# Six fields of the second tile loaded in parts of 39, 40 and 49 rows, and later loads in two pieces of 8 KB

## The chip, the cores and the metric

One core of a Trainium2 chip runs the kernel. The metric is the device time of one execution in microseconds, lower being better. The time before is 1293.61 us (median of 3 runs, 1291.99 to 1294.53). Other chips give the same kernel medians up to 1297.1 us, so every comparison below is with runs of the kernel before on the same chip in the same rounds. Where a kernel has a single run, its time is used only as a hint.

## The reference

```python
def _L0_rec_ref(x, W):                       # x: 4096 x 32 x 64, W: 64 x 64, float32
    vid = jnp.einsum('bfd,de->bfe', x, W)
    idx_i, idx_j = jnp.triu_indices(32, k=1)  # 496 pairs i < j
    return x[:, idx_i, :] * vid[:, idx_j, :]  # 4096 x 496 x 64, 520 MB
```

One small matrix product, then 496 products of fields for each sample. The input is 33.6 MB, the output 520 MB.

## The kernel before

The batch is cut into 16 tiles of 256 samples: 128 partitions, 32 fields, 128 columns. TensorE makes `vid` in PSUM, VectorE multiplies into output tiles of 124 pairs, and SyncE's queue stores each of these. A full store is one transfer of 128 rows of 63,488 B.

```python
    xpool = ctx.enter_context(tc.tile_pool(name="x", bufs=2))
    opool = ctx.enter_context(tc.tile_pool(name="out", bufs=3))
    ...
    def load(t, pieces, queue):
        xt = xpool.tile([P, F, C], F32, tag="x", name=f"x_{t}")
        n = F // pieces
        for lo in range(0, F, n):
            queue.dma_start(out=xt[:, lo : lo + n, :], in_=x[t][:, lo : lo + n, :])
        return xt

    loaded = [load(0, 4, nc.sync), load(1, 2, nc.sync)]
    ...
    for t in range(NT):
        if 0 < t < NT - 1:
            loaded.append(load(t + 1, 4, nc.scalar))
        xt = loaded[t]
        ...  # matmuls of the tile into PSUM
        for at, m, w, i, di, j, dj in products(by_field() if t < 2 else by_block()):
            ...
            nc.vector.tensor_tensor(o, left, right, ALU.mult)
            at += n
            if t * NP + at == until or at in (base + SLOT, NP):
                nc.sync.dma_start(
                    out=out[t][:, sent:at, :],
                    in_=ot[:, sent - base : at - base, :],
                )
```

The first two tiles are loaded on SyncE's queue. From tile 2 on ScalarE's queue loads the next tile as soon as an x buffer is free, in four pieces of 8 fields, 4 KB per partition.

## Time and profile before

| | before |
|---|---|
| median time, us | 1293.61 |
| profiled span, us | 1293.4 |
| bytes moved, MB | 553.8 |
| VectorE busy | 84% |
| DMA engines busy | nine tenths or more in 39 of 40 slices |

The table of DMA issues below (transfer, issuing queue, count, KB of one, median us from issue to landing) shows that a store waits behind another one, as it lands in 43 us but takes 20, and that a load piece needs about as long in the median:

```profile
out_dram<-o SPq DMA_DIRECT2D x56, 7936.0 KB, 43.1
x<-in_r_x_dram ACTq DMA_DIRECT2D x56, 512.0 KB, 45.5
```

The **excess** of a store packet is its duration above the 2342 ns that undisturbed packets of 63,488 B take. The **lag** of a DMA engine is how long after the first of the 16 engines it finishes the same store, read from the 16 completion writes. The **spread** is the lag of the last engine at the last store. Packet durations and completion writes are in the DMA records of each trace.

### The profile page before, as it was taken

How to read it: one execution, taken by the hardware profiler on the slowest of the kernel's cores; microseconds unless marked ns; L12 is line 12 of the kernel's file. 1: busy time of each engine (PE TensorE's matmuls, PEld its weight loads, DVE VectorE, ACT ScalarE, POOL GpSimd, SP SyncE). 2: the span in 40 equal slices, each digit the busy share in tenths (PEclk: the TensorE clock that was granted, in tenths of full speed). 3: DMA queues.
4: the chain of work that ended last, by engine and by line, in shares of the span. 5: the costliest groups of instructions: out<-in, count | busy, mean ns of one | idle time of the engine just before them, and what ended most of it. 6: DMA issues, size and time to landing. Idle time of an engine off the chain costs nothing.

```text
span 1293.4 us, 1789 instructions
## 1 busy us (share of the span) xinstructions
PE 227.8 (18%) x512; PEld 48.5 (4%) x512; DVE 1083.6 (84%) x320; POOL 0.2 (0%) x4
## 2 busy tenths in 40 slices
PE   4112122112122121221212212122121221212000
PEld 1000000000000000000000000000000000000000
DVE  7999999888898887888879788798887988979870
POOL 0000000000000000000000000000000000000000
PEclk7555555555555565555555556555565555555555
DMA  9999999999999999999999999999999999999996
GB/s 393 429 423 438 429 432 435 430 431 434 433 434 431 432 433 435 433 435 436 433 431 436 431 433 431 435 434 431 431 431 434 431 433 427 427 431 438 438 430 302
DMA packets 20889, 553.80 MB, mean 428 GB/s; under 512 B 2448, under 2 KB 2448, under 8 KB 10256
## 3 DMA queue, kind: packets, MB, share of 16 engines
q1 hardware_dynamic: 12816, 524.33, 93.9%
q10 hardware_dynamic: 8064, 29.36, 5.6%
q8 instruction: 4, 0.07, 0.0%
q14 instruction: 5, 0.04, 0.0%
HBM read 33.59 MB, written 520.09 MB: 428 GB/s over the span
## 4 chain that ended last, share of the span: by engine, by line
DMA 55%; DVE 39%; issue 2%; PE 0%; DVEq 0%; SPq 0%
DMA out_dram<-o 55%; DVE o L159 39%; DMA x<-in_r_x_dram 0%; PE vid L134 0%; DVEq L200 0%; DVEq L159 0%; SPq L111 0%
## 5 line engine op out<-in xcount | busy, mean ns | idle before, releaser
L159 DVE TENSOR_TENSOR o<-x,vid 128x2048 f32<-128x2048 f32 (+13 forms) x320 | 1083.6, 3454 | 170.0 <-DMA out_dram<-o 124.2
L134 PE MATMUL vid<-x,w 64*64 64x512 f32 x512 | 227.8, 1025 | 958.6 <-DMA x<-in_r_x_dram 629.4
L134 PEld LDWEIGHTS vid<-x,w 64*64 64x64 f32 x512 | 48.5, 205 | 1136.2 <-DVE o L159 572.9
L182 POOL MEMSET const-bfloat16-1.0<- 128x1 bf16 x1 | 0.1, 102 | 0.0
L182 POOL MEMSET const-uint8-127<- 128x1 uint8 x1 | 0.1, 101 | 0.0
L182 POOL MEMSET const-float32-0.0<- 128x1 f32 x1 | 0.1, 99 | 0.2 <-issue 0.2
L182 POOL MEMSET const-float32-1.0<- 128x1 f32 x1 | 0.1, 98 | 0.0
## 6 DMA issues: line engine op xcount, KB each, us to landing
out_dram<-o SPq DMA_DIRECT2D x56, 7936.0 KB, 43.1
x<-in_r_x_dram ACTq DMA_DIRECT2D x56, 512.0 KB, 45.5
out_dram<-o SPq DMA_DIRECT2D x2, 3008.0 KB, 17.7
out_dram<-o SPq DMA_DIRECT2D x1, 5952.0 KB, 26.9
out_dram<-o SPq DMA_DIRECT2D x1, 4928.0 KB, 23.1
out_dram<-o SPq DMA_DIRECT2D x1, 4416.0 KB, 19.0
out_dram<-o SPq DMA_DIRECT2D x1, 4224.0 KB, 21.2
out_dram<-o SPq DMA_DIRECT2D x1, 3904.0 KB, 15.3
```

Source lines behind the costliest of these rows:

```text
L134: nc.tensor.matmul(vid[half, b : b + BANK, :], lhsT=w2[half, :], rhs=xt[half, b : b + BANK, :], start=True, stop=True,)
L159: nc.vector.tensor_tensor(o, left, right, ALU.mult)
L182: nc = _bacc.Bacc("TRN2", target_bir_lowering=False, num_devices=1, dynamic_dma_scratch_size=1024)
```

## The change

Its intent is to load with fewer and larger packets, and to shift some of the second tile's bytes between DMA engines.

```diff
-    loaded = [load(0, 4, nc.sync), load(1, 2, nc.sync)]
+    loaded = [load(0, 4, nc.sync)]
+
+    x1 = xpool.tile([P, F, C], F32, tag="x", name="x_1")
+    for p, q, lo, hi in ((0, P, 6, F), (0, 39, 0, 6), (39, 79, 0, 6), (79, P, 0, 6)):
+        nc.sync.dma_start(out=x1[p:q, lo:hi, :], in_=x[1][p:q, lo:hi, :])
+    loaded.append(x1)
...
-            loaded.append(load(t + 1, 4, nc.scalar))
+            loaded.append(load(t + 1, 2, nc.scalar))
```

## The prediction

> **What bounds the kernel now.** I read the page first, then the waits, then the time windows of the start and the end, and last the single DMA packets in the trace. The page:
>
> ```profile
> PE 227.8 (18%) x512; PEld 48.5 (4%) x512; DVE 1083.6 (84%) x320; POOL 0.2 (0%) x4
> ...
> DMA  9999999999999999999999999999999999999996
> ...
> DMA packets 20889, 553.80 MB, mean 428 GB/s; under 512 B 2448, under 2 KB 2448, under 8 KB 10256
> ...
> q1 hardware_dynamic: 12816, 524.33, 93.9%
> q10 hardware_dynamic: 8064, 29.36, 5.6%
> ```
>
> VectorE is busy 84%, but the 16 DMA engines are at nine tenths or more in 39 of 40 slices, the last one apart. Queue 1 has the stores and the loads of the first two tiles; queue 10 has the loads of tiles 2 to 15, which ScalarE's queue issues. So 520 of 554 MB are output, and the change touches the other 6%. The waits between 200 and 1200 us say the same:
>
> ```profile
> DVE o L159 <- DMA out_dram<-o: 120.3, 38, 4.0
> DVE o L159 <- issue: 38.1, 12, 4.2
> ```
>
> VectorE waits for output buffers to be stored, never for x or for TensorE in this stretch. TensorE's own 575 us of waiting for x costs nothing as long as VectorE has products to make. Now windows of the late part; the last two columns are the DMA share and GB/s:
>
> ```profile
> 600.00:1180.00 580.00, 106.82 (x232) 22.13 (x228) 486.13 (x129) 0.00 (x0) 0.54 1.00 433
> 1180.00:1240.00 60.00, 3.62 (x8) 0.84 (x8) 54.05 (x15) 0.00 (x0) 0.53 1.00 434
> 1240.00:1280.00 40.00, 0.00 (x0) 0.00 (x0) 13.60 (x4) 0.00 (x0) 0.50 1.01 440
> 1280.00:1284.00 4.00, 0.00 (x0) 0.00 (x0) 0.00 (x0) 0.00 (x0) 0.50 0.48 206
> 1284.00:1288.00 4.00, 0.00 (x0) 0.00 (x0) 0.00 (x0) 0.00 (x0) 0.50 0.26 111
> 1288.00:1293.00 5.00, 0.00 (x0) 0.00 (x0) 0.00 (x0) 0.00 (x0) 0.50 0.03 13
> ```
>
> The engines are full until about 1282 us, and then come 10 us in which only some work: 0.48, 0.26 and 0.03 of them. The 16 completion writes of the last store, one from each DMA engine, tell how many. Seven come at 1282.1 to 1282.3 us, four at 1283.7 to 1283.8, and five at 1287.8, 1288.1, 1288.5, 1289.0 and 1292.2. Their mean is 1284.7, so with equal work the last byte would land 7.5 us earlier. **The span is set by the DMA engine that falls furthest behind.**
>
> Where does it fall behind? I followed the distance from the first to the sixteenth completion write, store by store. It is 0.8 us at 79 us (before the first load of queue 10), 2.2 at 251, 4.6 at 550, 7.0 at 830 and 10.6 at 1169. After 1188, when no load is left, it stays at 10.2 for the last six stores. So the lag grows only while loads run beside stores. The packets show it too: a store packet of 63,488 B takes 2342 ns nearly always, but between 200 and 1180 us some 9% take 3 to 200 ns more, 31 us of engine time in all. Following the packets engine by engine (a reconstruction, as the records do not name the engine), four or five engines have most of it, 3 to 7 us each. Between 1185 and 1282 us the same excess is 0.1 us. The load packets themselves are steady at 159 ns. Nine instruction fetches also land on single engines: four of 16 KB at 0.88 to 0.96 us and five of 8 KB at 0.31 us.
>
> **What the Trainium skill says.** "DMA: Bandwidth & Descriptors", section "Queues, rings and completion order": each DMA engine goes round-robin between the queues it has work for, one packet at a time. The trace agrees: in the steady part each engine alternates one 2342 ns store packet with one 159 ns load packet. The same page, section "Why a DMA increments its semaphore by 16 and not by 1": a transfer runs on the largest number of engines up to 16 that divides its row count, and for this kind of queue on the lowest-numbered ones. The trace before has only transfers of 128 rows, each with 16 completion writes, which agrees but does not test other counts. The same page, section "Why small descriptors are slow (HBM only)": each packet carries a fixed overhead. The trace agrees: 4,096 B take 159 ns and 8,192 B take 309, so the fixed part is 2 x 159 - 309 = 9 ns. The same page, section "Specifications": a fabric ceiling of 435 GB/s. The trace has 2342 ns for 63,488 B, 27.1 GB/s on each of 16 engines, 434 together, so no engine can be made faster.
>
> **The change part by part.**
>
> *Later loads in two pieces.* Fourteen tiles lose two of their four loads: 28 transfers fewer. Data packets of queue 10 fall from 14 x 4 x 128 = 7168 to 3584, completion writes from 896 to 448; the bytes stay. Consecutive packets of one engine overlap by 3 to 4 ns in the records, so an 8 KB packet really saves 2 x (159 - 3.5) - (309 - 3.5) = 5.5 ns. 3584 x 5.5 = 19.7 us, and 448 completion writes of 9 - 3 = 6 ns are 2.7 us. The sum, 22.4 us over 16 engines, is **1.4 us**, and it lies on the bound, as every engine is always busy.
>
> *When the loads run.* Before, an engine has 32 load packets and 32 store packets per tile, one to one, so loads are in flight for the whole of a tile's 80 us. After, 16 load packets are spent beside 16 store packets: 16 x (2.34 + 0.31) = 42 us, then 38 us of stores alone. If the excess of store packets comes with the time in which loads are in flight, it halves. Of the slowest engine's 9 us of lag gained since 170 us, I put some 1 to 2 to instruction fetches and 7 to the excess; half is 3.5 us. If it comes with the bytes loaded, nothing changes. I choose between the two: **2.5 us**.
>
> *x landing earlier.* The last piece landed up to 81.9 us after its issue, and should now need some 45. TensorE will wait less for x, but VectorE was not waiting for x and the DMA engines were never without work: worth 0.
>
> *The second tile in parts.* By the rule above 39 rows go on 13 engines with 3 rows each, 40 on 10 with 4, 49 on 7 with 7; a row is 6 x 512 = 3 KB. Engines 0 to 6 get 14 rows or 42 KB, 7 to 9 get 21 KB, 10 to 12 get 9 KB, 13 to 15 nothing, where each had 8 rows or 24 KB. The total is the same. At 27.1 GB/s that is 18 KB or 0.68 us more on the lowest seven and 24 KB or 0.9 us less on the top three. It is a deliberate head start for some engines, so it gains up to 0.9 us if the worst engine is among the top three, and costs up to 0.7 if it is among the lowest seven. The change looks tuned on the chip, so I take a gain of 0.2 to 0.3. The two added issues, near 0.43 us each on the issuing queue, fall at 4 us, before the first store is ready at 11 us: hidden.
>
> Sum: 1293.6 - 1.4 - 2.5 - 0.2 = **1289.5 us**.
>
> **Rivals.** *First, the transfers are hidden work and only the 1.4 us shows*: the excess moves with the bytes, because an 8 KB load disturbs a store twice as long as one of 4 KB. For it: the excess is an effect of both kinds of traffic, and their amounts are unchanged. Against it: nothing that I see. About 1292 us. *Second, the head start decides the lag*: engines that begin 0.7 us behind meet the other engines' loads at other phases, and the lag grows faster or slower than before. For it: the late packets are mostly the eighth of a store, on engines already behind. Against it: 10 us of lag after 1188 us cause no excess. It can make anything from 1285 to 1295. *Third, a new wait*: loads of 8 KB take 0.31 of 2.65 us, 12%, of an engine's time in the first half of a tile instead of 6%, stores land later there, VectorE waits longer for a buffer and then the engines run dry. Against it: a store lands 43 us after issue and takes 20 us, so a second one is always queued, and VectorE needs 67 us (1084 / 16) of a tile's 80. I give it 3%; it would make some 1300 us.
>
> **Range and chances.** A bound on the gain is all imbalance gone and all overhead saved, 7.5 + 1.4 = 9 us or 0.7%, so 2% faster is out of reach. The runs of before spread over 2.5 us. I take 1285.5 to 1294.0 us, and chances of 0.01, 0.98 and 0.01.
>
> **What would show it right or wrong.** Packets of queue 10 should fall to 4032 and their share of the engines from 5.6% to about 5.4%. ACT-issued loads should be 28 of 1024 KB with a median landing near 30 us. TensorE's waits for x should shrink. The DMA row should stay at 9, VectorE's waits for stores should stay near 120 us, and the 10 us ramp of the last windows should shorten to some 6 to 8 us. The prediction is wrong if the ramp stays or grows while the packets fall (first or second rival), or if the DMA share dips below 1.00 in mid-run (third).

## The result, and the profile after

The changed kernel takes 1300.76 us (median of 4 runs, 1300.52 to 1304.73) against 1294.07 us (4 runs) for the kernel before: a ratio of 1.0058, 95% interval 1.0032 to 1.0085. A ratio here is always the mean of one kernel's fast runs over the mean of the other's fast runs of the same rounds, so it differs a little from the ratio of the medians. The change is within 2%, as forecast, but slower, and outside the forecast range of 1285.5 to 1294.0 us. That it stayed within 2% says little for the reasoning, as the direction was wrong.

The page of the changed kernel:

```profile
PE 208.8 (16%) x512; PEld 48.0 (4%) x512; DVE 1083.7 (83%) x320; POOL 0.2 (0%) x4
...
DMA  9999999999999999999999999999999999999995
...
DMA packets 16870, 553.79 MB, mean 425 GB/s; under 512 B 2014, under 2 KB 2014, under 8 KB 2782
...
q1 hardware_dynamic: 12830, 524.33, 93.6%
q10 hardware_dynamic: 4032, 29.36, 5.3%
...
out_dram<-o SPq DMA_DIRECT2D x56, 7936.0 KB, 43.2
x<-in_r_x_dram ACTq DMA_DIRECT2D x28, 1024.0 KB, 26.6
```

Everything that the change was to do, it did: 4032 packets on queue 10, a share of 5.3%, loads that land in 26.6 us. The DMA row is still full. VectorE's time is the same, and it waits longer for stores. Between 200 and 1200 us:

```profile
PE vid L139 <- DMA x<-in_r_x_dram: 270.7, 12, 23.3
DVE o L164 <- DMA out_dram<-o: 165.6, 49, 5.8
```

The wait of 165.6 us, 120.3 before, is no new bound: counted from the packets, fewer than 16 were in flight for 0.2 us of engine time in all between 82 us and the first engine's end. No engine ran dry while VectorE waited. The windows of the end show where the time is (DMA share and GB/s last):

```profile
1200.00:1280.00 80.00, 0.00 (x0) 0.00 (x0) 57.61 (x13) 0.00 (x0) 0.50 1.00 432
1280.00:1284.00 4.00, 0.00 (x0) 0.00 (x0) 0.00 (x0) 0.00 (x0) 0.50 0.88 381
1284.00:1288.00 4.00, 0.00 (x0) 0.00 (x0) 0.00 (x0) 0.00 (x0) 0.50 0.33 143
1288.00:1293.00 5.00, 0.00 (x0) 0.00 (x0) 0.00 (x0) 0.00 (x0) 0.50 0.29 127
1293.00:1303.00 10.00, 0.00 (x0) 0.00 (x0) 0.00 (x0) 0.00 (x0) 0.50 0.09 38
```

The ramp in which only some engines work was 10 us long and is now 19. The completion writes of the last store agree: the first engine is done at 1283.0 us (1282.1 before), the last at 1301.7 (1292.2 before). So 0.9 us of the 9.5 us between the two profiled spans are in the first engine's end and 8.5 in the spread, 18.7 for 10.2. Five engines are more than 10 us behind. (The profiled run is the slowest of the four; the medians differ by 6.7 us.)

The excess of full store packets between 200 and 1180 us is 86.1 us of engine time, 30.8 before. Nearly all of it lies in the stretches in which loads run: summed in steps of 20 us from 220 us on it goes, for example, 2.4, 1.1, 0.0 and 0.1 us, then 2.8, 3.7, 0.0 and 0.0. That it comes and goes with the loads is thus visible in the trace; that there is more of it in half the time is the surprise.

### The profile page after: what moved, and what is told of

It reads as the page before. It is cut to its first block, busy times and chain, and to the rows that moved or that the text cites.

```text
span 1302.9 us, 1734 instructions
## 1 busy us (share of the span) xinstructions
PE 208.8 (16%) x512; PEld 48.0 (4%) x512; DVE 1083.7 (83%) x320; POOL 0.2 (0%) x4
## 3 DMA queue, kind: packets, MB, share of 16 engines
q1 hardware_dynamic: 12830, 524.33, 93.6%
q10 hardware_dynamic: 4032, 29.36, 5.3%
## 4 chain that ended last, share of the span: by engine, by line
DMA 60%; DVE 35%; issue 2%; PE 0%; DVEq 0%; SPq 0%
DMA out_dram<-o 60%; DVE o L164 35%; DMA x<-in_r_x_dram 0%; PE vid L139 0%; DVEq L205 0%; DVEq L164 0%; SPq L111 0%
## 5 line engine op out<-in xcount | busy, mean ns | idle before, releaser
L139 PE MATMUL vid<-x,w 64*64 64x512 f32 x512 | 208.8, 954 | 983.1 <-DVE o L164 668.8
## 6 DMA issues: line engine op xcount, KB each, us to landing
x<-in_r_x_dram ACTq DMA_DIRECT2D x28, 1024.0 KB, 26.6
```

The lines of the kernel that those rows point to most:

```text
L139: nc.tensor.matmul(vid[half, b : b + BANK, :], lhsT=w2[half, :], rhs=xt[half, b : b + BANK, :], start=True, stop=True,)
```

## The experiments

Each spread and each excess is read from one profiled execution of a kernel, so a difference of a few us between two of them can be chance. The numbers e1 to e19 are the labels of the runs; there is no e18.

**The two halves of the change.** Theory A: the larger load packets hold stores up more. Theory B: the parts of the second tile put engines out of step, and that sets off the lag.

Parts alone (e1), later loads in four pieces:

```diff
-            loaded.append(load(t + 1, 2, nc.scalar))   # against the changed kernel
+            loaded.append(load(t + 1, 4, nc.scalar))
```

> Only the second tile in parts of 39, 40 and 49 rows; later loads in four pieces as before. Theory A (the loads of 8 KB make the lag grow): 1294 us give or take 2, the last store's 16 completion writes spread over 9 to 11 us as before, excess of store packets between 200 and 1180 us near 31 us. Theory B (the head start of 1.4 us between engines sets off the lag): about 1300 us, spread near 18 us.

Measured: 1297.36 us against 1297.1, ratio 1.0008 (0.9992 to 1.0025). Excess 32.4 us. The spread of 13.7 us is above the 9 to 11 expected; the profiled run is the slowest of the four. The parts do put engines out of step: at the first store seven engines are 1.4 to 2.0 us behind the first in the changed kernel. But at 80 us the whole spread is 0.9 us in this kernel and 1.2 in the changed one, 0.8 before. The head start is worn off before the first later load.

Two pieces alone (e2):

```diff
-            loaded.append(load(t + 1, 4, nc.scalar))
+            loaded.append(load(t + 1, 2, nc.scalar))
```

> Only the later loads in two pieces of 8 KB; second tile loaded as before. Theory A: about 1300 us, spread of the last completion writes near 18 us, excess of store packets near 86 us. Theory B: 1290 to 1292 us, spread 6 to 10 us.

Measured: 1300.83 us, ratio 1.0027 (1.0003 to 1.0052); excess 97.6 us, spread 14.3. The ends of the two profiles, the parts alone first, then two pieces alone:

```profile
1280.00:1284.00 4.00, 0.00 (x0) 0.00 (x0) 0.00 (x0) 0.00 (x0) 0.50 0.77 333
1284.00:1288.00 4.00, 0.00 (x0) 0.00 (x0) 0.00 (x0) 0.00 (x0) 0.50 0.18 79
1288.00:1293.00 5.00, 0.00 (x0) 0.00 (x0) 0.00 (x0) 0.00 (x0) 0.50 0.18 76
```

```profile
1280.00:1284.00 4.00, 0.00 (x0) 0.00 (x0) 0.00 (x0) 0.00 (x0) 0.50 0.92 397
1284.00:1288.00 4.00, 0.00 (x0) 0.00 (x0) 0.00 (x0) 0.00 (x0) 0.50 0.44 190
1288.00:1293.00 5.00, 0.00 (x0) 0.00 (x0) 0.00 (x0) 0.00 (x0) 0.50 0.47 203
```

With two pieces nearly half of the engines still work between 1288 and 1293 us, with the parts alone fewer than a fifth. The last engine alone does not tell these two profiles apart, as the spreads are 14.3 and 13.7 us. The sum of the lags of all 16 engines at the last store does: it is 42.8 us before, 45.1 with the parts alone, 63.3 to 91.8 in the four profiles with two pieces, and 107.2 with the one piece of 16 KB tried below. The excess goes the same way: 30.8, 32.4, 69.7 to 97.6, and 128.1 us.

To see whether the parts add to the loss of the pieces, both kernels ran again on one chip, five rounds each (e11 is the changed kernel, e12 the two pieces alone).

> The changed kernel as it is, on the same chip as e12_two_again, to see whether the parts of the second tile add to the loss. If they do nothing: the same time as e12_two_again within 2 us, both 3 to 7 us above before. If they do: 3 us or more above it.

> Two pieces of 8 KB without the parts, again: 3 to 7 us above before, spread of the last completion writes 12 to 19 us.

Measured: 1301.16 and 1300.66 us against 1295.09, both with ratio 1.0046 (1.0030 to 1.0061 and 1.0031 to 1.0061). Spreads 15.2 and 14.5 us, excess 69.7 and 80.1 us. **The loss is that of the two pieces; the parts do nothing that can be seen.**

**The size of a load packet.**

```diff
-            loaded.append(load(t + 1, 4, nc.scalar))
+            loaded.append(load(t + 1, 1, nc.scalar))   # e4; 8 pieces in e3
```

> The kernel before with one piece of 16 KB for each later load. Theory A: worse than two pieces, 1303 to 1310 us, spread over 20 us. Theory B: 1290 to 1292 us.

> The kernel before with eight pieces of 2 KB for each later load. Theory A says that smaller load packets disturb the stores less, and 7168 more packets at 5.5 ns cost 2.6 us over 16 engines, while the spread at the end should fall below 10 us: 1290 to 1295 us. In theory B the loads' size costs its overhead alone: 1296 to 1297 us with the spread unchanged. One thing can break this: with 64 load packets for 32 store packets per engine and tile, the loads may not land in time; then VectorE waits for TensorE and it is over 1310 us.

One piece (e4): 1301.79 us, ratio 1.0043 (1.0020 to 1.0065), a little under the expected range; excess 128.1 us, spread 14.8 and not over 20. So from 8 KB to 16 KB neither the time (e2 in the same rounds: ratio 1.0027) nor the spread went up clear of noise. The dose shows in the hold-ups themselves. Counting as slow a full store packet with more than 20 ns of excess:

| load packet | kernel | slow, of some 6,260 | median excess of a slow one, ns | load packet's own time, ns | all excess, us |
|---|---|---|---|---|---|
| 4 KB | before | 300 | 86 | 159 | 30.8 |
| 8 KB | two pieces again | 455 | 137 | 309 | 80.1 |
| 8 KB | changed | 473 | 139 | 309 | 86.1 |
| 16 KB | one piece | 471 | 245 | 611 | 128.1 |

A hold-up grows with the load packet, though less than in proportion, and 82% to 94% of them are no longer than one load packet. There are half as many load packets at each step, and yet not fewer hold-ups. The other two profiles with 8 KB have 519 (two pieces, first time) and 391 (changed kernel again) slow packets.

Eight pieces (e3): 1325.66 us, ratio 1.0229. This was the danger written down before: a load of 64 packets per engine needs 64 turns beside a tile's 32 stores, so x comes late and the engines run dry. The GB/s of the 40 slices:

```profile
GB/s 388 429 300 430 368 436 411 437 428 398 444 436 421 430 390 438 394 440 444 400 450 392 438 434 408 422 410 421 432 423 420 436 438 417 397 451 432 430 430 399
```

The drops to 300 and 368 are a shortage of work, 209 us of idle engine time in all. It says nothing about small packets. One thing is worth noting: the spread at the end is 0.5 us. Engines that ran out of work here were in step again afterwards.

**No loads, and loads that do not read HBM.**

```diff
-            loaded.append(load(t + 1, 4, nc.scalar))
+            loaded.append(loaded[1])                    # e6: wrong result on purpose
```

> Wrong result on purpose: tiles 2 to 15 use the second tile's x, nothing is loaded after it. Theory A: excess of store packets under 1 us between 200 and 1130 us, the spread stays near 1 to 2 us plus instruction fetches, and the time is that of the stores alone: 1294 less 7168 x 155.5 ns / 16 = 70 us less about 7 us of lag, some 1217 us. If the lag has nothing to do with loads, the spread still grows to 10 us and it is about 1224 us.

Measured: 1219.55 us (ratio 0.9414), spread 1.6 us, no engine over 2 us behind. Without later loads the lag does not grow, and the time is what the stores cost. A detail was off: the excess was 44 us and not under 1 us, but in many small amounts (the median store packet took 2347 ns and not 2342; above 2347 it is 21 us), and no engine falls behind by it, as the spread shows.

```diff
-            loaded.append(load(t + 1, 4, nc.scalar))
+            xt = xpool.tile([P, F, C], F32, tag="x", name=f"x_{t + 1}")
+            for lo in range(0, F, F // 2):
+                nc.scalar.dma_start(
+                    out=xt[:, lo : lo + F // 2, :], in_=loaded[t][:, lo : lo + F // 2, :])
+            loaded.append(xt)                           # e7: wrong result on purpose
```

> Wrong result on purpose: later tiles copy x in SBUF from the other buffer, in two pieces of 8 KB per partition, on ScalarE's queue, with the packets and times of e2_two_only but no read of HBM. If the hold-up comes from reading HBM beside writing it, the excess of store packets falls from 97 us to under 10 us. If it comes from writing SBUF beside reading it, it stays at 60 us or more.

The packets are those of the two-piece kernel, 3584 of 8 KB and 309 ns, in the same stretches of each tile, but they read SBUF. The spread is 1.4 us and the single run took 1290.05 us. The end of its profile:

```profile
1280.00:1284.00 4.00, 0.00 (x0) 0.00 (x0) 0.00 (x0) 0.00 (x0) 0.50 1.03 444
1284.00:1288.00 4.00, 0.00 (x0) 0.00 (x0) 0.00 (x0) 0.00 (x0) 0.50 0.15 64
```

All engines are at work up to 1284 us, and then all end within two. The excess is 60.5 us, so by the letter of the expectation the sign of the rival (writing SBUF beside reading it: 60 us or more) came out, and not that of reading HBM (under 10). But the excess is of another kind: the median store packet took 2349 ns, above which 28.5 us are left, slow packets have a median excess of 26 ns over 2342, and no lag comes of it. What decides is the spread, which the expectation did not name: 1.4 us here, in one profile, for 14.3 to 18.7 in the four profiles of two pieces from HBM. **The lag needs loads that read HBM; the excess as a sum does not.**

These traces also allow a comparison without a further run. For each store packet of 200 to 1160 us I took the time in which six or more load packets were in flight. (The limits of six packets and 300 ns are a choice.) With none of it, a store packet's mean excess was 1.1 ns in the changed kernel (3334 packets). With over 300 ns of it, it was 96.4 ns (666 packets), 72.9 in the two-piece kernel run again and 126.8 with one piece. In the copy from SBUF it was 9.5 ns without and 9.8 ns with (412 packets). This fits the following: a store packet is held when many engines read HBM at once, and it meets that moment only on an engine that is out of step with the many, as an engine in step is itself loading then. This is a reading of the traces and not shown by intervention; the next experiments tried to.

The counterpart, reading HBM but not writing SBUF, failed twice:

```diff
+            nc.scalar.copy(tick, ot[:, 0, 0:1])                    # e19 alone
+            for lo in range(0, F, F // 2):
+                nc.scalar.dma_start(out=scratch[t + 1][:, lo : lo + F // 2, :],
+                                    in_=x[t + 1][:, lo : lo + F // 2, :])   # e8, e19: HBM to HBM
```

> Wrong result on purpose: later tiles use the second tile's x, while the same 28 transfers of 1 MB go from HBM to a scratch array in HBM, all issued early, so in the first 600 to 700 us. If the hold-up comes from reading HBM, stores in that stretch still have excess, 60 us or more in all. If it comes from writing SBUF, the excess is under 10 us.

> e8 without its fault: there the 28 transfers had all ended at 163 us, before the first store packet of full size, so it tested nothing. Here ScalarE first reads one element of the tile's last output buffer, so each tile's two copies from HBM to HBM, 8 KB packets, run beside full stores as the loads of e2_two_only do. Wrong result on purpose. If reading HBM together with the others is enough to hold stores up: excess of store packets 60 us or more between 200 and 1180 us, and a spread over 8 us. If it takes loads that go into SBUF: under 25 us and a spread under 3 us, as in e7_from_sbuf.

Spreads were 2.3 and 2.1 us, times of the single runs 1291.09 and 1290.28 us, but the copies ran between 2 and 163 us in the first and 2 and 171 us in the second, before and beside the small early stores only; the first store packets of 63,488 B came at 235 us. In the second I had relied on ScalarE reading an output tile first; the transfers to scratch did not wait for that: 20 of the 28 were issued before the first such read. Neither tests the question, and it stays open whether the write into SBUF is needed too.

**The order of loads and stores (e5).**

```diff
-            loaded.append(load(t + 1, 4, nc.scalar))
+            loaded.append(load(t + 1, 4, nc.sync))
```

> The kernel before with the later loads, four pieces, issued by SyncE on the queue of the stores, so that each engine does a load's packets in a run, after the stores already queued, and no longer one load packet after each store packet. Theory A (a store packet is held up when some engine's load packet falls into it, by up to that packet's length): most store packets then run beside stores alone, the excess of store packets falls well below 31 us, the spread of the last completion writes below 6 us, time 1286 to 1290 us against about 1294 to 1297. Rival (the lag comes from the amount loaded, wherever it lies): excess and time as before. Rival (stores wait behind loads in one queue, engines or VectorE run dry): over 1297 us.

Measured: 1302.6 us, ratio 1.0056 (1.0035 to 1.0077), spread 13.6. It was no shortage of work, as the engines were idle for 4.9 us in all. Stores had 16.9 us of excess only, as expected, but the spread did not shrink. The load packets, steady at 159 ns before, now had 60 us of excess, in 306 of 7168. The queue's share shows that all is one queue now:

```profile
q1 hardware_dynamic: 20880, 553.69, 99.3%
```

The hold-up moved from the stores to the loads. My expectation that loads in a run would disturb less was wrong.

**Engines pushed out of step on purpose.** Theory C: many loads at once hold back the few stores that run then, so engines spread evenly would not be held. Theory D: an engine out of step is slower, so any push makes more lag. The numbers of engines below rest on the rule of the row count that the prediction cites.

```diff
+        for n in (16, 15, 14, 13, 12, 11, 10, 9, 8, 7, 6, 4, 3):     # tile 4 only; e9, e10, e15
+            queue.dma_start(out=xt[p : p + n, 0:12, :], in_=x[t][p : p + n, 0:12, :])
+            p += n
```

> The kernel before, with 12 fields of tile 4's load cut into parts of 16, 15, 14 and so on to 3 rows, so that engine 0 gets 13 rows of 6 KB and engine 15 one: a ramp of about 2.7 us over the engines, as long as one store packet plus one load packet. Theory C (stores of engines out of step are held while many engines, in step, load from HBM at the same moment): the engines' loads then fall at different moments, six or more at once hardly ever, the excess of store packets after 300 us falls to a few us, the spread of the last completion writes stays at 3 to 5 us, time 1286 to 1291 us where before has 1294 to 1297. Rival D (any lag makes more lag, the engine behind is the one that suffers): the ramp starts it earlier, spread over 12 us, 1297 to 1302 us.

> The same ramp with the later loads in two pieces of 8 KB. Theory C: excess of store packets from 97 us down to under 25, spread under 7 us, 1285 to 1291 us, at least 8 us below e12_two_again. Rival D: 1300 us or more.

Measured (e9, e10): 1299.59 and 1304.42 us, ratios 1.0033 (1.0019 to 1.0048) and 1.0070 (1.0056 to 1.0084). They look like theory D, but the condition was not met: the extra load packets of the low engines made tile 4's x late, the engines were idle for 41 and 37 us in all, and one store after the ramp the spread was down to 0.6 and 0.5 us. The spreads then grew to 11.7 and 14.9, as in the kernels without a ramp (10.2, and 14.3 to 18.7). These runs tell nothing of C or D.

The next three carry marks: tiny loads of 16 down to 2 rows behind the last store.

```diff
+    for n in range(16, 1, -1):                         # e13, e14, e15
+        nc.sync.dma_start(out=mark[:n, 17 * (n - 1) : 17 * (n - 1) + n + 1],
+                          in_=x[0][:n, 0, 0 : n + 1])
```

```diff
+        for n in 16 * (8,):                            # e14, tile 4: parts of 8 rows
+            queue.dma_start(out=xt[p : p + n, 0:6, :], in_=x[t][p : p + n, 0:6, :])
+            p += n
```

In e14 and e15 the rest of tile 4's load is one transfer.

> The kernel before, and behind its last store fifteen tiny loads of 16, 15 and so on down to 2 rows, each of its own packet size. A load of n rows runs on the n lowest engines if the rule of the row count holds, so the number of tiny packets behind an engine's last store names the engine. It tells which engines are behind at the end. Time within 2 us of before; five or so engines 5 to 12 us behind. No theory says which numbers they have.

> The marks, and tile 4's load of six fields cut into sixteen parts of 8 rows, which puts all of it on engines 0 to 7: a push of 0.9 us back for these and 0.9 us forward for engines 8 to 15 at about 230 us, without a shortage of work as the rest of that load is one piece. Theory D (out of step with the others means slower, so lag feeds on itself): engines 0 to 7 fill most of the lag at the end, six or more engines over 5 us behind, time 1297 to 1303 us. If the slow engines are slow by their place: the same numbers as in e13_marks are behind, 1295 to 1297 us.

> The ramp of e9 without its fault: there the parts and four further pieces needed more turns than a tile has stores, x came late, the engines ran dry for 41 us of engine time in all and were in step again afterwards. Here the rest of tile 4's load is one piece. No idle engine time, a ramp of up to 2.7 us seen in the completion writes near 280 us. Theory C (many simultaneous loads hold back the stores out of step): six or more loads at once are rare afterwards, excess of store packets under 15 us from 300 us on, spread at the end under 6 us, 1287 to 1292 us. Theory D: spread over 12 us, 1297 us or more.

(One correction to the last text: e9 had three further pieces, not four.) The single run of e13 took 1297.15 us, within 2 us of before as expected, but two engines and not five or so were over 5 us behind. Each load of n rows had exactly n packets, and the ends nest, so the marks work for n from 10 to 16; smaller ones were issued too late. If the n engines are the lowest, the engine that takes part in 15 rows but not in 14 has number 14. It is the last in e13 (8.5 us behind) and in e14 (10.2 us), and 4.5 us behind in e15, where the last is one of engines 0 to 9. In e14, at least four of the six engines that are 5 us or more behind, 11 to 14, are among 8 to 15, which had been pushed forward: the opposite of theory D. In e15, engines 10 to 13 and 15 are within 0.2 us of the first. So in these three executions neither "the same engines always" nor "those pushed back" holds. Times were 1302.63 us (ratio 1.0054) and 1301.56 us (1.0048), but again the engines ran short at tile 4, 44 and 26 us in all, and the first engine's end moved from 1282.1 to 1286.5 and 1285.2 us; the spreads, 10.2 and 9.8, are those of before. The slice at 227 to 260 us (the eighth number) of the ramp kernel e15 has the shortage:

```profile
GB/s 392 430 426 433 439 437 431 392 440 426 435 432 431 434 431 433 431 433 431 431 431 430 431 433 432 433 432 433 430 434 431 428 431 427 434 430 441 438 436 262
```

Which engines fall behind, and what puts them out of step first, I could not settle.

**Load packets under 4 KB (e16, e17).** To leave room for more turns, each full store was issued as two transfers of half the packet.

```diff
+                mid = (sent + at) // 2
+                for lo, hi in ((sent, mid), (mid, at)) if at - sent == SLOT else ((sent, at),):
                     nc.sync.dma_start(out=out[t][:, lo:hi, :], ...)
...
+            loaded.append(load(t + 1, 6, nc.scalar))    # e17: 5 x 3 KB + 1 KB; e16: 8 x 2 KB
```

> The kernel before with each full store issued as two transfers of half the packet (31,744 B) and each later load in eight pieces of 2 KB: loads still alternate one to one with stores and last for the whole tile, but an interfering load packet is half as long (84 ns and not 159). Overhead: 448 more store and 448 more load packets per engine at 5.5 ns, 5 us. If the hold-up of a store is up to one load packet long: mean hold-up of slow store packets near 50 ns and not 93, excess about 15 to 30 us, spread at the end 5 to 8 us, time 1293 to 1297 us. If it has nothing to do with the length: spread 10 us, 1299 to 1301 us.

> e16 without its fault: there 64 turns of 1.27 us per tile were 82 us, more than a tile has, and x came late. Here six pieces, five of 3 KB and one of 1 KB per partition: 48 turns, 61 us. If a store is held up by at most one load packet: mean hold-up of slow store packets 60 to 80 ns, spread at the end 6 to 9 us, no idle engine time, 1292 to 1296 us with 2.5 to 3 us more overhead than before. If the hold-up does not go with the load packet's length below 4 KB: spread 10 us or more, 1297 to 1301 us.

Eight pieces of 2 KB ran dry again (340 us of idle engine time): 1335.13 us, ratio 1.0307. A 2 KB load packet took 98 ns on average rather than 84, which the 82 us of turns had no room for.

Six pieces ran almost without a shortage (1.4 us of idle engine time): the spread is 4.7 us, no engine is over 5 us behind, and only 62 of 12,521 store packets have more than 20 ns of excess, 15 us in all. Where the two-piece kernel has a long ramp, this one is full until 1288 us:

```profile
1280.00:1284.00 4.00, 0.00 (x0) 0.00 (x0) 0.00 (x0) 0.00 (x0) 0.50 0.98 421
1284.00:1288.00 4.00, 0.00 (x0) 0.00 (x0) 0.00 (x0) 0.00 (x0) 0.50 0.97 421
1288.00:1293.00 5.00, 0.00 (x0) 0.00 (x0) 0.00 (x0) 0.00 (x0) 0.50 0.15 63
```

What remains of hold-ups is not what I expected: few, often on several engines in the same microsecond, and with a mean of 196 ns and not 60 to 80. And the time is no better, 1296.55 us against 1294.82 (20 and 23 runs, ratio 1.0033, 1.0011 to 1.0054), as the first engine ends 5.8 us later, at 1287.9 us: the added packets cost about what the spread gives back. As store packets and load packets were both made smaller, the gain cannot be put down to the loads alone. The median is of all 20 runs; five took 1304 to 1317 us, and why is open: the profile is of one of the quick runs. The 15 quick ones have a mean of 1296.5 us, 1.3 us above the mean before. No kernel that I ran and that computes the right result beats the one before.

## Why the prediction was right or wrong

*That the DMA engines are the bound, and that the slowest of them sets the end*, held. It accounts for the loss: first end and spread add up to the difference of the spans.

*Overhead of 1.4 us saved.* The counts came out exactly, 3584 data packets of 309 ns on queue 10. The gain does not show in the end: the first engine ends 0.9 us later, not 1.4 us earlier, and 0.4 to 1.7 us later in the other four profiles with two pieces or one. The packet records after 82 us tell where it went. As a mean over the 16 engines, load packets and completion writes took 2.5 us less than before, but packets overlapped each other 1.5 us less, so about 1.0 us was saved. Store packets took 4.2 us more, and the mean engine ends 3.2 us later.

***When the loads run* is the step that failed.** I put it that the excess "comes with the time in which loads are in flight" and "halves", or else "with the bytes loaded, nothing changes", and took 2.5 us of gain. It does come almost only while loads are in flight, and that time did halve. But what it amounts to per unit of that time is not a constant: a slow store packet is mostly held for no longer than a load packet takes, and with the doubled packet the hold-up was longer (median 86 to 139 ns), and the slow ones became more, not fewer (300 to 473; 391 to 519 in the other profiles with two pieces). The excess went from 30.8 to 86.1 us and the spread from 10.2 to 18.7 us. The first rival, "an 8 KB load disturbs a store twice as long as one of 4 KB", had the mechanism but assumed half as many hold-ups; its 1292 us fell with that.

*x landing earlier is worth 0*: right. TensorE's waits for x fell from 575.0 to 270.7 us and nothing became faster.

*The second tile in parts*: the split over engines was right. Queue 1 has 12,830 packets for 12,816, that is 14 more completion writes: 16 for the full part and 13 + 10 + 7 = 30 for the three others, where two transfers had 32. The push was seen in the first store, but wore off by 80 us. Its gain of 0.2 us was a guess at the wrong effect, and the second rival, that it decides the lag, fell with e1, which was no slower than before, and with e11 and e12, which had the same ratio of 1.0046.

*The third rival*, engines running dry, did not occur here (0.2 us of engine time). Engines did run dry, for 26 to 340 us of engine time, in e3, e9, e10, e14, e15 and e16, where loads needed more turns or came late. One small reading was off: nine of the slow store packets before took over 200 ns more, up to 479.

The range was too narrow on the slow side because I allowed only for less disturbance or the same. That twice the time per packet gives more packets held fits with many engines reading HBM at once, but this is argued from the traces and not shown; why particular engines fall out of step is open.

## What to carry to other kernels

When all DMA engines are full, look at the completion writes of the last transfer: the last engine sets the time, not the mean. A small stream of loads beside a large stream of stores can cost more through the lag that it makes than through its packet overhead (before, the last engine ended 7.5 us after the mean one, and the overhead to be saved was estimated at 1.4 us), and larger load packets can make that worse, so measure the spread before making packets larger. Smaller packets are no free cure either: with the queues alternating as here each load packet needs a turn, and when the turns ran out (e3, e16) the engines ran dry.

## What the Trainium skill lacked or had wrong

- "DMA: Bandwidth & Descriptors", section "Why small descriptors are slow (HBM only)", gives what small packets cost. No page gives a measured cost of larger load packets for stores on another queue: here a store excess of 30.8 us for load packets of 4 KB, 69.7 to 97.6 for 8 KB and 128.1 for 16 KB, and a slower kernel (ratio 1.0046 for 8 KB, twice, and 1.0043 for 16 KB).
- No page tells that the DMA engines of a core drift apart when ordinary loads from HBM run beside stores: 8.5 to 18.7 us at the end of the profiles with loads of 4 to 16 KB whose engines did not run dry, and 1.6 us without later loads.
- "DMA: Bandwidth & Descriptors", section "Latency and other measured facts", has engines 7 and 15 as usually slower and gives the software path as a best guess. All transfers of this kernel are on hardware queues, so this does not contradict it. Here the engine that the marks name as 14 was last in two of three marked executions, 8.5 and 10.2 us behind; 15 was at most 2.1 us behind, and 7 could not be told.
